# A cross-attention and state-space layer: loads before the main loop in another order, chunks of keys fetched seven ahead, the context's mean from longer rows

## The chip, the cores and the metric

The kernel runs on one core of a Trainium2 chip. The metric is the device time of one execution in microseconds (us); lower is better. The value before is the median of three runs. Where a stage is looked at, the figures come from one profiled execution, whose own time is given beside its span.

## The reference

The reference takes `x` (4096 rows of 512), a context `ctx` (3202 rows of 512), a second context `ctxb` (3202 rows of 64) and weights. All is float32. In short:

```python
xn  = layernorm(x, g1, beta1)
cn  = layernorm(ctx, g1, beta1)
q, k, v = heads(xn @ Wq.T + bq), heads(cn @ Wk.T + bk), heads(cn @ Wv.T + bv)   # 8 heads of 64
x1  = x + softmax(q @ k.T / 8) @ v @ Wo.T + b_o
u   = (layernorm(x1, g2, beta2) @ W_in.T + b_in) @ Bmat                          # 4096 x 64
s_t = silu(s_(t-1) @ A.T) + u_t                                                  # a scan over the rows
out = x1 + s @ Cmat + mean(ctxb, over its rows) @ W_prog.T + b_prog
```

The change concerns how `ctx`, `ctxb`, the weights and the first rows of `x` are brought in, before the attention proper starts.

## The kernel before, in words

The kernel has three stages: the preparation of K, V and the first block of Q; the attention, with the projections and the input of the scan as background work; and the scan with the output. The change lies in the first stage alone.

**Chunks and groups.** The context is cut into 26 chunks of 124 or 123 rows (`keys(c)`: 124 for the first four, 123 after), and chunks go in groups of four, so there are six full groups and one of two chunks. For each chunk, `load_chunk` brings the rows into a tile `cx` (SP's queue), `norm_chunk` takes its statistics on DVE (L111, L113), makes the scale and shift on POOL (L115 to L119) and the normalized rows `xh` on ACT (L125). `turn_chunk` transposes `xh` on TensorE (`tp_c`, L136) and copies it into the group's tile `ct`, by ACT for even chunks and by DVE for odd ones. Four pairs of matmuls make the V rows `pv` (L390); ACT copies them to `vs` (three buffers) and SP stores them to `vd` in DRAM (L400). After the last chunk of a group, four K products `pk` (L415) go through ACT to `ks` (three buffers, L423) and are stored by SP to `kd` (L428), two stores for each. The attention reads `kd` and `vd` back in tiles.

**Order.** The stage stands under `manual_schedule`, so each engine and each queue carries out its instructions in the order in which the program issues them. In iteration `c` the order is: load of chunk `c + 4`, normalization of chunk `c + 3`, V product of chunk `c`, transposes of chunk `c + 2`, copy and store of V of chunk `c`, and at a group's end the K products and stores. A load thus stands on SP's queue behind the V stores, and behind the K stores, that were issued before it. The tile `cx` has five buffers.

**Side work.** The generators `first` and `side` yield between small steps, and the loop takes a step of one of them in each iteration and after each K product (`next`). They fold the layer norm's gain and shift into the weights (`gain`, `shift`, `pr`, `pb`), fold `W_in` and `Bmat` into one matrix (`pw`, `pt`, `wc`), take the mean of `ctxb` (`cb`, `sums`, `pm`, `mean`), add constant rows (`rowb`, `modb`), and make the first block of Q (`queries(0)`: loads of `x`, `tp_x`, `pq`). Their loads go by ACT's queue, those of `x` by SP's. What is left of `side` after the loop is carried out there.

**Completion of loads and stores.** In the built program the loads and stores of both queues take eight completion semaphores in turn. An issue that takes a semaphore waits until the load or store that had it before is complete, whichever queue that one was on.

The lines that matter most: `load_chunk` (L345 to L350), the loads ahead of the loop (L366 to L374), the loop (L383 to L430), `fetch_w` (L199), the load of `ctxb` (L252 to L259) with its reduces (L305 to L313), the loads of `x` in `queries` (L155).

Of the kernel before, what the change touches and what calls it, by code (L numbers as in the profile page):

```python
# [8 lines left out]
F32 = mybir.dt.float32  # L9
# [3 lines left out]
ALU = mybir.AluOpType  # L13
# [10 lines left out]
GC = 4  # L24
# [21 lines left out]
def xattn_ssm_kernel(  # L46
# [97 lines left out]
    ps_m = actx.enter_context(tc.tile_pool(name="ps_m", bufs=2, space=PSUM))  # L144
    qt = {}

    def queries(Q):

        xns = []
        for half in range(2):  # L150
            xn = xnp.tile([P, NC, QU], F32, tag="xn", name=f"xn_{Q}_{half}")
            xns.append(xn)
            for t in range(NT // 2):
                r = Q * QB + half * QU + t * P
                xt = xp_.tile([P, H], F32, tag="x", name=f"x_{r}", bufs=3)  # L155
                nc.sync.dma_start(xt, x[r : r + P, :])
                yield False
                scaled = normalize(xt, P, f"x{r}", later=True)
                yield False
                yield False  # L160
                xh = scaled()
                yield False
                tp = transposes(ps_m, "m", xh, P, f"x{r}")
                yield True
                nc.scalar.copy(xn[:, :, t * P : (t + 1) * P], tp)
                yield False
                yield False
        for hp in range(NC):
            pq = ps_m.tile([P, 512], F32, tag="m", name=f"pq_{Q}_{hp}")
            for half in range(2):  # L170
                for i in range(NC):
                    nc.tensor.matmul(  # L172
                        pq[:, half * QU : (half + 1) * QU],
                        wq[:, i, hp * P : (hp + 1) * P],
                        xns[half][:, i, :],
                        start=(i == 0),
                        stop=(i == NC - 1),
                    )
            yield True
            t = qp.tile([P, QB], F32, tag="q", name=f"q_{Q}_{hp}")  # L180
            nc.scalar.activation(
                t, pq, AF.Identity, bias=bias[:, hp : hp + 1], scale=HD**-0.5
            )
            qt[Q, hp] = t
            yield False
# [10 lines left out]
    wv = wp.tile([P, NC, H], F32, name="wv")  # L196
    raw = [wp.tile([P, NC, H], F32, name=f"raw_{k}") for k in "qkv"]

    def fetch_w(k):  # L199
        nc.scalar.dma_start(raw[k], wsrc[:, :, k * H : (k + 1) * H])  # L200

    def gain(k, w):
        for i in range(NC):
            nc.vector.tensor_scalar(
                w[:, i, :], raw[k][:, i, :], g1s[:, i : i + 1], None, ALU.mult
            )
# [27 lines left out]


    def side():
        fetch_w(0)
        yield from shift(2)
        nc.scalar.dma_start(wo, wo_t.rearrange("(c p) o -> p c o", p=P))
        yield  # L240
        gain(0, wq)
        yield from shift(0)

        nc.vector.tensor_scalar(bias[:, :NC], bias[:, :NC], HD**-0.5, None, ALU.mult)

        win = wp.tile([P, NC, H], F32, name="win")
        nc.scalar.dma_start(win, w_in.rearrange("(c p) i -> p c i", p=P))
        bm = wp.tile([P, NC, NS], F32, name="bm")
        nc.scalar.dma_start(bm, bmat.rearrange("(c p) s -> p c s", p=P))
        bi = wp.tile([P, NC], F32, name="bi")  # L250
        nc.scalar.dma_start(bi, b_in)
        cb = wp.tile([CK, NCH, NS], F32, name="cb")  # L252
        a = GC * CK
        nc.scalar.dma_start(
            cb[:, :GC, :], ctxb[:a, :].rearrange("(c p) d -> p c d", p=CK)
        )
        nc.scalar.dma_start(
            cb[: CK - 1, GC:, :], ctxb[a:, :].rearrange("(c p) d -> p c d", p=CK - 1)
        )  # L259
        for _ in range(6):  # L260
            yield

        nc.scalar.dma_start(rowb, b_o.rearrange("(a h) -> a h", a=1).to_broadcast([P, H]))
        nc.scalar.dma_start(modb, b_prog.to_broadcast([P, H]))
        wp_t = wp.tile([NS, H], F32, name="wp_t")
        nc.scalar.dma_start(wp_t, wprog_t)
        for k in (0, NS):
            nc.scalar.dma_start(a_t[k : k + NS, k : k + NS], at)
        pw = ps_m.tile([P, 512], F32, tag="m", name="pw")
        for c in range(NC):  # L270
            nc.tensor.matmul(
                pw[:NS, :], bm[:, c, :], win[:, c, :], start=(c == 0), stop=(c == NC - 1)
            )
        yield
        wct = wp.tile([NS, H], F32, name="wct")
        nc.vector.tensor_copy(wct, pw[:NS, :])
        yield
        pt = ps_m.tile([P, NC, P], F32, tag="m", name="pt")
        for i in range(NC):
            nc.tensor.transpose(  # L280
                pt[:, i, :NS], wct[:, i * P : (i + 1) * P], ident[:NS, :NS]
            )
        yield
        wcr = wp.tile([P, NC, NS], F32, name="wcr")
        nc.vector.tensor_copy(wcr, pt[:, :, :NS])
        for i in range(NC):
            nc.vector.tensor_scalar(
                wc[:, i, :], wcr[:, i, :], g2s[:, i : i + 1], None, ALU.mult
            )
        yield  # L290
        pb = ps_m.tile([P, 512], F32, tag="m", name="pb")
        for c in range(NC):
            nc.tensor.matmul(
                pb[:NS, 0:1], bm[:, c, :], bi[:, c : c + 1], start=(c == 0), stop=False
            )
        for i in range(NC):
            nc.tensor.matmul(
                pb[:NS, 0:1], wcr[:, i, :], be2s[:, i : i + 1], start=False, stop=(i == NC - 1)
            )
        yield  # L300
        for k in (0, NS):
            nc.vector.tensor_copy(bu[k : k + NS], pb[:NS, 0:1])

        sums = wp.tile([CK, 2, NS], F32, name="sums")
        nc.vector.tensor_reduce(  # L305
            sums[:, 0, :], cb[:, :GC, :].rearrange("p c d -> p d c"), AX.X, ALU.add
        )
        nc.vector.tensor_reduce(
            sums[: CK - 1, 1, :],
            cb[: CK - 1, GC:, :].rearrange("p c d -> p d c"),  # L310
            AX.X,
            ALU.add,
        )  # L313
        yield
        pm = ps_m.tile([P, 512], F32, tag="m", name="pm")
        for i, n in enumerate((CK, CK - 1)):
            nc.tensor.matmul(
                pm[:NS, 0:1], sums[:n, i, :], ones[:n, 0:1], start=(i == 0), stop=(i == 1)
            )
        yield  # L320
        mean = wp.tile([NS, 1], F32, name="mean")
        nc.vector.tensor_scalar(mean, pm[:NS, 0:1], 1.0 / S2, None, ALU.mult)
        yield


        for dst, terms in (
            (modb, [(mean, wp_t)]),
            (rowb, [(bias[:, 2 * NC + c : 2 * NC + c + 1], wo[:, c, :]) for c in range(NC)]),
        ):
            pr = ps_m.tile([P, 512], F32, tag="m", name="pr")  # L330
            for i, (left, right) in enumerate(terms):
                nc.tensor.matmul(
                    pr, left.to_broadcast([left.shape[0], P]), right,
                    start=(i == 0), stop=(i == len(terms) - 1),
                )
            yield
            nc.vector.tensor_tensor(dst, pr, dst, ALU.add)
            yield
        yield from queries(0)

# [2 lines left out]
    def load_chunk(c):  # L345
        if c < NCH:
            n = keys(c)
            xt = cin.tile([CK, H], F32, tag="cx", name=f"cx_{c}", bufs=5)
            nc.sync.dma_start(xt[:n], ctx_in[key0(c) : key0(c) + n, :])
            cxs[c] = xt  # L350

# [13 lines left out]
    with tc.manual_schedule():  # L365
        load_chunk(0)  # L366
        nc.scalar.dma_start(g1s, g1)
        fetch_w(2)
        load_chunk(1)
        for t, src in ((be1s, beta1), (bqkv, b_qkv), (g2s, g2), (be2s, beta2)):  # L370
            nc.sync.dma_start(t, src)
        load_chunk(2)
        fetch_w(1)
        load_chunk(3)  # L374
        norm_chunk(0)
        norm_chunk(1)
        turn_chunk(0)
        gain(2, wv)
        turn_chunk(1)
        norm_chunk(2)  # L380
        work = side()
        first = shift(1)
        for c in range(NCH):  # L383
            load_chunk(c + 4)
            norm_chunk(c + 3)
            g, n = c // GC, keys(c)
            ct, o = cts[g], key0(c) - key0(g * GC)
# [13 lines left out]
                vd[:, c // 2, :n, c % 2, :].rearrange("h p d -> p h d"), vs[:n]  # L401
            )
            if c < GC:
                if c == 0:
                    gain(1, wk)
                next(first)
            else:
                next(work, None)
            if c % GC < GC - 1 and c < NCH - 1:
# [2 lines left out]
            for hp in range(NC):  # L412
# [13 lines left out]
                for b in range(g * GC, c + 1, 2):  # L426
                    m, k = 2 * keys(b), key0(b) - key0(g * GC)
                    nc.sync.dma_start(kd[hp, b // 2, :, :m], ks[:, k : k + m])  # L428
                for _ in range(2 if g > 2 else 1):
                    next(work, None)  # L430
        left = sum(1 for _ in work)
        assert left < 12, left
    prep.close()
    lctx = ExitStack()
    ps_s = lctx.enter_context(tc.tile_pool(name="ps_s", bufs=2, space=PSUM))
# [533 lines left out]
```

## Time and profile before

| | |
|---|---|
| time, median of three runs | 2682.13 us (2678.46 to 2682.83) |
| time of the profiled execution | 2679.33 us |
| its span in the profile | 2677.4 us |
| granted TensorE clock, mean | 0.977 of full speed |
| PE busy in the span | 2507.3 us, 94% |
| DVE, ACT, POOL busy | 80%, 69%, 77% |
| DMA, mean rate | 66 GB/s |
| first scores of the attention (L460) | at 304.84 us |

The profile gives, for each engine, the busy time; "busy tenths" show the span in 40 equal slices. PE is TensorE's matmuls and PEld its weight loads, DVE the vector engine, ACT the scalar engine, POOL GpSimd, SP the engine whose queue issues most of the loads and stores. A wait is named by who waited and for whom ("DVE st_c L111 <- DMA cx": the statistics waited for a chunk's load). `SPq` and `ACTq` are the issues on the two queues. The granted clock is what the throttle left of TensorE's full speed. The share of DMA is the mean over 16 engines.

### The profile page before, as it was taken

How to read it: one execution, taken by the hardware profiler on the slowest of the kernel's cores; microseconds unless marked ns; L12 is line 12 of the kernel's file. 1: busy time of each engine (PE TensorE's matmuls, PEld its weight loads, DVE VectorE, ACT ScalarE, POOL GpSimd, SP SyncE). 2: the span in 40 equal slices, each digit the busy share in tenths (PEclk: the TensorE clock that was granted, in tenths of full speed). 3: DMA queues.
4: the chain of work that ended last, by engine and by line, in shares of the span. 5: the costliest groups of instructions: out<-in, count | busy, mean ns of one | idle time of the engine just before them, and what ended most of it. 6: DMA issues, size and time to landing. Idle time of an engine off the chain costs nothing.

```text
span 2677.4 us, 44182 instructions
## 1 busy us (share of the span) xinstructions
PE 2507.3 (94%) x16588; PEld 1424.4 (53%) x16588; DVE 2146.1 (80%) x2321; ACT 1836.0 (69%) x2085; POOL 2065.1 (77%) x1170
## 2 busy tenths in 40 slices
PE   7788799999999999999999999999999999999957
PEld 3333555555565556555555556555555565555533
DVE  2121298899979998999989897999799979999825
ACT  2122387787878787877878787878687878788610
POOL 1111099899979998999979897999799979999870
PEclk9889999999999999999999999999999999999976
DMA  4332221112212221122111221212112211221043
GB/s 123 90 92 85 77 67 45 46 57 68 70 41 58 59 75 47 53 67 70 58 50 56 81 60 43 61 52 82 33 55 69 69 42 58 58 65 54 27 147 126
DMA packets 167551, 176.62 MB, mean 66 GB/s; under 512 B 16701, under 2 KB 140645, under 8 KB 167335
## 3 DMA queue, kind: packets, MB, share of 16 engines
q1 hardware_dynamic: 155374, 158.21, 20.0%
q10 hardware_dynamic: 11961, 15.54, 1.9%
q8 instruction: 134, 2.20, 0.3%
q14 instruction: 82, 0.67, 0.1%
HBM read 143.81 MB, written 29.89 MB: 65 GB/s over the span
## 4 chain that ended last, share of the span: by engine, by line
PE 44%; DVE 26%; issue 18%; ACT 8%; POOL 3%; DMA 2%; SPq 0%; ACTq 0%; DVEq 0%; POOLq 0%
DVE top L481 17%; PE s L460 14%; PE po L543 12%; DVE p L515 5%; PE pq L172 4%; ACT p L470 4%; PE pa L628 4%; ACT p L525 2%; PE tt L492 2%; PE py_c L871 1%; DVE rd L600 1%; PE mb L507 1%; PE pu L660 1%; PE pk L415 1%; POOL acc L534 1%
## 5 line engine op out<-in xcount | busy, mean ns | idle before, releaser
L534 POOL TENSOR_TENSOR acc<-p,acc 123x1024 f32<-123x1024 f32 x698 | 1657.0, 2374 | 115.3 <-ACT p L525 73.8
L470 ACT COPY p<-s 123x1024 f32<-123x1024 f32 (+1 forms) x832 | 834.2, 1003 | 274.1 <-PE s L460 263.4
L515 DVE TENSOR_TENSOR p<-p,mb 123x1024 f32<-123x1024 f32 (+1 forms) x832 | 1001.2, 1211 | 0.8 <-PE mb L507 0.8
L460 PE MATMUL s<-q,k 64*123 64x256 f32 (+1 forms) x6656 | 940.0, 401 | 61.0 <-DVE top L481 50.6
L525 ACT ACTIVATE p<-p 123x1024 f32<-123x1024 f32 (+1 forms) x832 | 880.1, 1058 | 143.7 <-DVE p L515 137.1
L481 DVE TENSOR_TENSOR top<-s,top 123x1024 f32<-123x1024 f32 x704 | 856.7, 1217 | 139.4 <-ACT p L470 130.6
L543 PE MATMUL po<-p,v 123*64 123x256 f32 (+1 forms) x6656 | 901.3, 392 | 1.1 <-ACT o L586 0.9
L460 PEld LDWEIGHTS s<-q,k 64*123 64x123 f32 (+1 forms) x6656 | 559.3, 181 | 373.6 <-DVE top L481 172.5
L543 PEld LDWEIGHTS po<-p,v 123*64 123x64 f32 (+1 forms) x6656 | 404.8, 136 | 399.4 <-issue 223.1
L534 POOL TENSOR_TENSOR acc<-p,p 124x1024 f32<-124x1024 f32 x64 | 151.9, 2374 | 152.6 <-ACT p L525 152.3
L115 POOL TENSOR_SCALAR ve_c<-mv_c 123x1 f32<-123x1 f32 (+1 forms) x26 | 6.1, 233 | 187.7 <-DVE mv_c L113 181.6
L111 DVE BATCH_NORM_STATS2 st_c<-cx 123x6 f32<-123x512 f32 (+1 forms) x26 | 18.0, 692 | 151.8 <-DMA cx<-in_ctx_dram 151.8
L628 PE MATMUL pa<-wo,o 128*128 128x512 f32 x256 | 119.5, 611 | 2.3 <-DVE x L637 2.3
L172 PE MATMUL pq<-xn,wq 128*128 128x256 f32 x512 | 117.9, 383 | 0.0
L481 DVE TENSOR_TENSOR top<-s,p 124x1024 f32<-124x1024 f32 x64 | 77.9, 1217 | 40.6 <-DMA k<-kd 39.3
L125 ACT ACTIVATE xh_c<-cx,nmr_c,rstd_c 123x512 f32<-123x512 f32 (+1 forms) x26 | 21.1, 812 | 129.1 <-POOL nmr_c L119 129.1
L172 PEld LDWEIGHTS pq<-xn,wq 128*128 128x128 f32 x512 | 95.0, 190 | 20.7 <-issue 6.3
L415 PE MATMUL pk<-ct,wk 128*128 128x492 f32 (+2 forms) x224 | 99.0, 599 | 3.3 <-ACT ks L423 3.3
L390 PE MATMUL pv<-wv,ct 128*123 128x512 f32 (+1 forms) x208 | 96.3, 607 | 0.0
L589 POOL TENSOR_TENSOR both<-acc 124x512 f32<-124x512 f32 x63 | 80.8, 1283 | 4.9
L499 DVE TENSOR_REDUCE m<-tt 128x2 f32<-128x496 f32 x128 | 79.9, 665 | 0.7 <-PE tt L492 0.7
L628 PEld LDWEIGHTS pa<-wo,o 128*128 128x128 f32 x256 | 46.8, 192 | 62.2 <-issue 56.3
(157 smaller groups left out, 1335.3 us busy)
## 6 DMA issues: line engine op xcount, KB each, us to landing
k<-kd SPq DMA_DIRECT2D x352, 123.0 KB
v<-vd SPq DMA_DIRECT2D x352, 123.0 KB
x<-in_x_dram SPq DMA_DIRECT2D x32, 256.0 KB
xr<-in_x_dram SPq DMA_DIRECT2D x32, 256.0 KB
out_dram<-row_c ACTq DMA_DIRECT2D x32, 256.0 KB
k<-kd SPq DMA_DIRECT2D x64, 124.0 KB
v<-vd SPq DMA_DIRECT2D x64, 124.0 KB
x1d<-x SPq DMA_DIRECT2D x28, 256.0 KB
```

The costliest lines, as they stand in the source:

```text
L172: nc.tensor.matmul(pq[:, half * QU : (half + 1) * QU], wq[:, i, hp * P : (hp + 1) * P], xns[half][:, i, :], start=(i == 0), stop=(i == NC ...
L390: nc.tensor.matmul(pv[:n, :H], ct[:, i, o : o + n], wv[:, i, :], start=(i == 0), stop=(i == NC - 1),)
L415: nc.tensor.matmul(pk[:, :n_g], wk[:, i, hp * P : (hp + 1) * P], ct[:, i, :n_g], start=(i == 0), stop=(i == NC - 1),)
L460: nc.tensor.matmul(s[:n, a, b, :], kts[(*w["at"][:2], c)][r, b * n : (b + 1) * n], q[r], start=True, stop=True,)
L470: nc.scalar.copy(t[:n], s[:n])
L481: nc.vector.tensor_tensor(w["top"][:n], s[:n], before[:n], ALU.max)
L515: nc.vector.tensor_tensor(t[:n], t[:n], w["mb"][:n].unsqueeze(2).to_broadcast([n, 2, 2, QU]), ALU.subtract,)
L525: nc.scalar.activation(t[:n], t[:n], AF.Exp)
L534: nc.gpsimd.tensor_tensor(w["acc"][:n], t[:n], before[:n], ALU.add)
L543: nc.tensor.matmul(w["po"][a * HD : (a + 1) * HD, 0, :], vts[(*w["at"][:2], c)][:n, b, a * HD : (a + 1) * HD], t[:n, a, b, :], start=(c == ...
L589: nc.gpsimd.tensor_tensor(both, acc[:, :, 0, :], acc[:, :, 1, :], ALU.add)
L628: nc.tensor.matmul(pa, o_t[Q, c][:, t * P : (t + 1) * P], wo[:, c, :], start=(c == 0), stop=(c == NC - 1),)
```

## The change

W_v is loaded in two halves, one by each queue. The chunks 1 to 3 and W_k are issued at once, the four small vectors after them, and chunks 4 to 6 ahead of the loop; in the loop, iteration `c` loads chunk `c + 7`, and `cx` has eight buffers. The gain of W_v stands ahead of the statistics of chunk 1, and gain and shift of W_k come one chunk later. The loads of `win`, `bm` and `bi` move ahead, that of `wo` later. `ctxb` is read as 128 partitions of 25 successive rows (6.4 KB each), with the last two rows in a tile of their own, and one reduce takes the place of two. The first 512 rows of `x` come in one load by ACT. The side work takes two steps after each K product from group 2 on, and is done when the loop ends.

```diff
@@ queries @@
-    def queries(Q):
+    def queries(Q, fetched=None):
...
-                xt = xp_.tile([P, H], F32, tag="x", name=f"x_{r}", bufs=3)
-                nc.sync.dma_start(xt, x[r : r + P, :])
-                yield False
+                if fetched:
+                    xt = fetched[:, half * (NT // 2) + t, :]
+                else:
+                    xt = xp_.tile([P, H], F32, tag="x", name=f"x_{r}", bufs=3)
+                    nc.sync.dma_start(xt, x[r : r + P, :])
+                    yield False
...
@@ fetch_w @@
-    def fetch_w(k):
-        nc.scalar.dma_start(raw[k], wsrc[:, :, k * H : (k + 1) * H])
+    def fetch_w(k, queue, part=slice(0, NC)):
+        queue.dma_start(raw[k][:, part], wsrc[:, part, k * H : (k + 1) * H])
...
@@ side @@
-        fetch_w(0)
+        fetch_w(0, nc.scalar)
         yield from shift(2)
-        nc.scalar.dma_start(wo, wo_t.rearrange("(c p) o -> p c o", p=P))
-        yield
-        gain(0, wq)
-        yield from shift(0)
-
-        nc.vector.tensor_scalar(bias[:, :NC], bias[:, :NC], HD**-0.5, None, ALU.mult)
 
         win = wp.tile([P, NC, H], F32, name="win")
         nc.scalar.dma_start(win, w_in.rearrange("(c p) i -> p c i", p=P))
...
-        cb = wp.tile([CK, NCH, NS], F32, name="cb")
-        a = GC * CK
-        nc.scalar.dma_start(
-            cb[:, :GC, :], ctxb[:a, :].rearrange("(c p) d -> p c d", p=CK)
-        )
-        nc.scalar.dma_start(
-            cb[: CK - 1, GC:, :], ctxb[a:, :].rearrange("(c p) d -> p c d", p=CK - 1)
-        )
-        for _ in range(6):
-            yield
+        gain(0, wq)
+        yield from shift(0)
+
+        cb = wp.tile([P, S2 // P, NS], F32, name="cb")
+        a = S2 // P * P
+        nc.scalar.dma_start(cb, ctxb[:a, :].rearrange("(p c) d -> p c d", p=P))
+        cb2 = wp.tile([S2 - a, NS], F32, name="cb2")
+        nc.scalar.dma_start(cb2, ctxb[a:, :])
+        x0 = wp.tile([P, NT, H], F32, name="x0")
+        yield
+
+        nc.vector.tensor_scalar(bias[:, :NC], bias[:, :NC], HD**-0.5, None, ALU.mult)
...
             nc.scalar.dma_start(a_t[k : k + NS, k : k + NS], at)
+        yield
+        nc.scalar.dma_start(wo, wo_t.rearrange("(c p) o -> p c o", p=P))
         pw = ps_m.tile([P, 512], F32, tag="m", name="pw")
...
-        sums = wp.tile([CK, 2, NS], F32, name="sums")
-        nc.vector.tensor_reduce(
-            sums[:, 0, :], cb[:, :GC, :].rearrange("p c d -> p d c"), AX.X, ALU.add
-        )
-        nc.vector.tensor_reduce(
-            sums[: CK - 1, 1, :],
-            cb[: CK - 1, GC:, :].rearrange("p c d -> p d c"),
-            AX.X,
-            ALU.add,
-        )
+        sums = wp.tile([P, NS], F32, name="sums")
+        nc.vector.tensor_reduce(sums, cb.rearrange("p c d -> p d c"), AX.X, ALU.add)
+        nc.scalar.dma_start(x0, x[:QB, :].rearrange("(t p) h -> p t h", p=P))
         yield
         pm = ps_m.tile([P, 512], F32, tag="m", name="pm")
-        for i, n in enumerate((CK, CK - 1)):
+        for i, t in enumerate((sums, cb2)):
+            n = t.shape[0]
             nc.tensor.matmul(
-                pm[:NS, 0:1], sums[:n, i, :], ones[:n, 0:1], start=(i == 0), stop=(i == 1)
+                pm[:NS, 0:1], t, ones[:n, 0:1], start=(i == 0), stop=(i == 1)
             )
...
-        yield from queries(0)
+        yield from queries(0, x0)
@@ load_chunk @@
-            xt = cin.tile([CK, H], F32, tag="cx", name=f"cx_{c}", bufs=5)
+            xt = cin.tile([CK, H], F32, tag="cx", name=f"cx_{c}", bufs=8)
...
@@ ahead of the loop, and the loop @@
         load_chunk(0)
         nc.scalar.dma_start(g1s, g1)
-        fetch_w(2)
+        fetch_w(2, nc.scalar, slice(0, NC // 2))
+        fetch_w(2, nc.sync, slice(NC // 2, NC))
         load_chunk(1)
+        load_chunk(2)
+        fetch_w(1, nc.scalar)
+        load_chunk(3)
         for t, src in ((be1s, beta1), (bqkv, b_qkv), (g2s, g2), (be2s, beta2)):
             nc.sync.dma_start(t, src)
-        load_chunk(2)
-        fetch_w(1)
-        load_chunk(3)
+        for c in range(4, 7):
+            load_chunk(c)
         norm_chunk(0)
-        norm_chunk(1)
         turn_chunk(0)
         gain(2, wv)
+        norm_chunk(1)
         turn_chunk(1)
         norm_chunk(2)
         work = side()
         first = shift(1)
         for c in range(NCH):
-            load_chunk(c + 4)
+            load_chunk(c + 7)
             norm_chunk(c + 3)
...
             if c < GC:
-                if c == 0:
+                if c == 1:
                     gain(1, wk)
-                next(first)
+                for _ in range((0, 1, 1, 2)[c]):
+                    next(first)
             else:
                 next(work, None)
...
-                for _ in range(2 if g > 2 else 1):
+                for _ in range(2 if g > 1 else 1):
                     next(work, None)
```

More of the change, by code (lines that the diff above doesn't have):

```diff
@@ L428, in xattn_ssm_kernel @@
                     nc.sync.dma_start(kd[hp, b // 2, :, :m], ks[:, k : k + m])
-                for _ in range(2 if g > 2 else 1):
+                for _ in range(2 if g > 1 else 1):
                     next(work, None)
         left = sum(1 for _ in work)
-        assert left < 12, left
+        assert left == 0, left
     prep.close()
```

## The prediction

> **What bounds the kernel now.** Read first the page's slices (40 of 67 us each: busy tenths, granted clock, DMA).
>
> ```profile
> PE   7788799999999999999999999999999999999957
> ...
> PEclk9889999999999999999999999999999999999976
> DMA  4332221112212221122111221212112211221043
> ```
>
> TensorE is at nine tenths from slice 6 on; the first four slices and a half, the preparation of K, V and the first Q, stand at 7 to 8. The diff touches only these. The PE timeline puts the first scores (L460) at 304.84 us. All before is the stage in question: PE is busy 247.0 us of it and idle 57.8. The 2372.6 us after it are taken as they are. Next the windows view, cut at the group borders (group = four chunks of keys: V, then K). Columns: window, length, busy us of PE, PEld, DVE, ACT, POOL with counts, granted clock, DMA share, GB/s.
>
> ```profile
> 17.07:58.60 41.53, 40.75 (x116) 17.82 (x117) 10.13 (x23) 9.33 (x15) 6.68 (x18) 1.00 0.33 101
> 58.60:96.40 37.80, 35.44 (x97) 15.66 (x96) 7.03 (x17) 7.99 (x13) 4.68 (x12) 0.95 0.40 124
> 96.40:155.30 58.90, 40.33 (x109) 17.76 (x107) 6.40 (x16) 9.93 (x17) 4.21 (x12) 0.86 0.31 88
> 155.30:197.50 42.20, 38.11 (x100) 17.26 (x100) 10.11 (x19) 9.58 (x16) 5.27 (x15) 0.92 0.25 81
> 197.50:234.85 37.35, 32.17 (x86) 15.07 (x85) 4.77 (x10) 9.59 (x16) 4.21 (x12) 0.91 0.27 86
> 234.85:278.50 43.65, 35.05 (x105) 17.88 (x104) 5.49 (x12) 11.11 (x18) 5.27 (x15) 0.96 0.25 75
> 278.50:304.80 26.30, 24.08 (x97) 18.01 (x96) 0.00 (x0) 5.35 (x10) 0.00 (x0) 1.00 0.15 44
> ```
>
> Group 2 (third row) takes 58.9 us at 0.86 clock, the others about 40. Who keeps PE idle: the list of waits, 0 to 330 us (total, times, longest).
>
> ```profile
> DVE st_c L111 <- DMA cx<-in_ctx_dram: 151.8, 23, 20.7
> ...
> PE tp_c L136 <- ACT xh_c L125: 42.6, 9, 10.6
> ...
> ACT ks L423 <- DMA bi<-in_L_xattn_b_in_dram: 9.4, 1, 9.4
> ```
>
> So: chunk load, then stats (DVE), POOL, ACT, then PE's transposes. Why are loads late? The DVE timeline shows chunks 16, 17, 18:
>
> ```profile
> 163.28 0.70 DVE L111 BATCH_NORM_STATS2 st_c<-cx 123x6 f32<-123x512 f32 x1 [4.44 <-DMA cx<-in_ctx_dram]
> ...
> 170.49 0.69 DVE L111 BATCH_NORM_STATS2 st_c<-cx 123x6 f32<-123x512 f32 x1 [5.67 <-DMA cx<-in_ctx_dram]
> ...
> 177.64 0.69 DVE L111 BATCH_NORM_STATS2 st_c<-cx 123x6 f32<-123x512 f32 x1 [6.13 <-DMA cx<-in_ctx_dram]
> ```
>
> One chunk lands every 7.15 us while PE needs 3.86 us for it (V matmuls start at 96.41, 100.27, 104.12). The DMA queue over 164 to 178 us (packets, MB, share of 16 engines), and SP's own waits:
>
> ```profile
> q1 hardware_dynamic: 1198, 0.99, 20.7%
> ```
>
> ```profile
> SPq L400 <- DMA cb<-in_ctxb_2048x_dram: 14.8, 1, 14.8
> ```
>
> A share of about 3/16 throughout, at 70 GB/s: three engines carry the chunk load and the V store.
>
> [...] `cb` is read in 256-byte pieces[...]; 4037 packets under 512 B pass between 92 and 132 us, and the window there has the long wait above. [...] after 8.09 us idle a V product took 4.86 us for 3.60.
>
> **Prices.** Chunk load 3.36 us of the three engines (chunks 3 and 4 land at 21.74 and 25.10, back to back), V store 7.15 − 3.36 = 3.8, landing latency 2.4 (an x load takes 3.1 from issue to use[...]). [...]
>
> **The change, part by part.**
>
> *Start.* W_v by two queues, chunks 1 to 3 and W_k at once instead of W_k at 7.44. The engines carry the same bytes until chunk 1, which still gates PE's second transpose: raw_v lands at about 10, chunk 1 at 13 (now 13.55). Gain 0.7 us; bounds −2 and +2 (W_k ahead in line). If W_v came after chunk 1, DVE would hold the stats of chunk 1 behind `gain`, which now stands ahead of them: that is the +2. The four small vectors now wait for chunk 0, W_v and `g1`; all are in by about 10, and they are first read at 23. SP's chunks 4 to 6 stand behind them: no loss, the engines are busy with chunks 2 and 3. `gain` and `shift` of W_k go one chunk later: the same 1.6 us on DVE and 3.6 + 1.0 on PE, costed at nothing, since the first K product is due only at 39 and W_k is in by 13; V products of chunks 1 to 3 cover them. If W_k came after 30, PE would wait in the `shift` by as much.
>
> *Context's mean.* [...] From issue (99) to SP's release (128.8) that load held chunks 12 to 14 back. Its reduces cost DVE 0.6 + 2.56 us; one of 1600 elements at the same rate costs 2.9. Group 2 loses its 18.6 us of idling (58.90 − 40.33).
>
> *Seven ahead.* A load is now issued four iterations before its stats instead of one. PE then pays its own work only: per chunk 3.86, per K product 3.35, plus the side work where the built program puts it. Group 0: 39.5 (41.53 less 0.78 idle and 1.3 of slow clock). Group 1: 4 x 3.86 + 4 x 3.35 = 28.8, shift of W_q 4.5 and `pw` 3.6: 36.9. Group 2: 28.8 and 7.3 (`pt`, `pb`, `pm` 1.8, the two `pr` 5.5): 36.1. Groups 3 and 4: 28.8 and two transposes of x: 29.8 each. The first Q product: 3.45. Group 5: 28.8 and three Q products 10.4: 39.2. Group 6: two V products 6.9, four short K products 6.6: 13.5. Sum 228.3. With a start at 17.3 and 2.3 for the first K load the scores begin at **247.9**, 57 us earlier. That is the floor: 39.6 us of idling (57.8 less 16 at the start and 2.3 at the end) and some 17 of slow clock (247.0 busy less 228.3, and 1 to 2 at the start that stay).
>
> *What is late next.* Four pairs and eight K stores hold the three engines 28.6 + 2.7 = 31.3 us a group. To the end of group 0 they have eleven loads: chunk 3 is through at 15.7, then 7 x 3.36 + 4 x 3.8 + W_q 2.8 + 2.7 and the landing 2.4 make 62; PE is done at 57. Group 1 adds `win`, `bm`, `cb` (6): 37.4 against 36.9. Group 2 adds `wo`, `rowb`, `modb`, `wp_t`, x (7.4): 38.7 against 36.1. Group 3: 31.3 against 29.8. The loads bear this, with four chunks in hand. The stores do not quite: SP is in order, so the first K store of a group issues behind its last V store, and the fourth `ks` (three buffers) waits for it on ACT, with `xh` of the chunk PE turns 7.7 us into the next group behind it. SP's lag, 5 to 9 us, passes that slack (7.7 less 1.6 for `ks` and `xh`) in groups 2 to 4 by 0 to 4 us each. Group 1 has a wait of its own: ACT issues `modb`, whose completion semaphore (eight go round) is that of V store 7, and `a_t`, that of the first K store. ACT stops at about 84 until 98, and `ks`, then `xh` of chunk 11 stand behind it: 2 us of PE. I take 8 us of stalls and 3 of slow clock. Bounds: 0, if they fit the slack, and 33 (second case).
>
> *x in one load.* 1 MB by ACT, in group 2, for four loads by SP: 2.8 us of the engines either way. PE's waits for x (6.9 us, in the idling above) go; four SP places at 0.44 go; ACT pays one issue, 0.4 us. `wo`, moved later, is read at the end of group 2, some 20 us after its issue; `win`, `bm`, `bi`, moved earlier, are read 25 us after theirs: nothing, with the V products of their group as cover.
>
> Sum: −57 + 11 = **−46 us**. The profiled execution took 2679.33 us, 1.93 beyond its span; the median of the runs is 2682.13, 0.1% above. Forecast 2682.1 − 46 = **2636**.
>
> **Rivals.**
>
> *The stores stay the bound.* SP waits for each `ks` in turn (kd stores take 13.2 us of SP in group 0), so loads and K phase would not overlap: 28.6 + 13.2 = 41.8 us in groups 1 to 3, 38.5 in group 4, then PE's 42.7 and 13.5. Scores at 58 + 125.4 + 38.5 + 56.2 + 2.3 = 280: −24, **2658**. For it: today's periods of 37 to 44. Against: today the loads are needed one iteration after issue; afterwards the engines can drain queued loads in the K phase.
>
> *ACT stands still* (slower). Five batches of loads on ACT each wait for a DMA eight places before, perhaps queued behind loads that nobody needs yet. Eight outstanding at 3.6 us are 29 us; less 8 of slack, 21 a time. Three such (63) outweigh 57 and leave 2682 + 6 = **2688**. For it: the 9.4 us wait for `bi` now. [...] It decides when ACT's blocks beyond the slack pass 57 us.
>
> *Nothing gained*: all stalls reappear in front of the stores; **2682**.
>
> **Numbers.** First case 0.68, stores 0.25, ACT 0.05, nothing 0.02. A measurement of this kernel can tell about 0.2% (5 us) from no change: faster 0.93, same 0.02, slower 0.05. Range 2622 (the floor and 3 us of scatter) to 2664 (the stores' case and 6).
>
> **What would show it.** Right: first scores at 255 to 262; no `cb` in SP's waits; group 2 near 40 us; DVE's wait for `cx` far below 151.8; clock near 1 from 96 to 220. ACT's `ks` waits for DMA should grow. Wrong: groups 1 to 3 still near 41 us with a DMA share of 0.19 throughout (the stores), ACT idle 20 us at a time before `ks` (third case), or a stage after the first scores that differs from 2372.6 us by over 5.

## The result, and the profile after

| | before | after |
|---|---|---|
| median of six runs, us | 2680.57 (2675.43 to 2685.05) | 2642.82 (2633.27 to 2649.38) |
| ratio, 95% interval | | 0.9858 (0.9834 to 0.9883) |
| profiled execution, its span | 2679.33, 2677.4 | 2643.80, 2642.0 |
| first scores of the attention | 304.84 (L460) | 263.32 (L459) |
| PE busy and idle ahead of them | 247.0, 57.8 | 234.0, 29.3 |
| stage after them | 2372.6 | 2378.7 |

The change makes the kernel faster by 1.4%. In the profiled executions the preparation is 41.5 us shorter: 28.5 us less of idle TensorE and 13.0 us less of busy time for the same products, at a granted clock of 0.99 where it was 0.94. These are the windows of the preparation, before and then after (columns as in the prediction: length; busy us of PE, PEld, DVE, ACT, POOL with counts; clock, DMA share, GB/s):

```profile
0.00:304.84 304.84, 247.02 (x707) 120.20 (x707) 47.52 (x107) 65.84 (x106) 33.54 (x97) 0.94 0.31 91
```

```profile
0.00:263.32 263.32, 233.97 (x707) 115.61 (x707) 46.27 (x106) 66.57 (x106) 32.87 (x97) 0.99 0.33 105
```

Next the page's slices of the kernel after (66 us each: busy tenths, granted clock, DMA).

```profile
PE   7989899999999999999999999999999999999857
...
PEclk9999999999999999999999999999999999999966
DMA  3422221112212121222112211222121312221133
```

The clock's first four digits were 9, 8, 8 and 9 and are all 9 now. The last two slices hold the end with the scan, which the diff doesn't touch; in the clock they are at 6 and 6 where they were at 7 and 6. The windows of the preparation after, cut at the group borders:

```profile
19.28:60.04 40.76, 40.76 (x113) 17.40 (x113) 12.22 (x29) 9.17 (x14) 6.71 (x18) 1.00 0.34 114
60.04:97.34 37.30, 37.30 (x106) 16.09 (x105) 6.10 (x15) 8.23 (x13) 4.47 (x14) 1.00 0.39 120
97.34:133.79 36.45, 35.78 (x115) 16.96 (x114) 10.76 (x23) 9.24 (x15) 4.18 (x12) 1.00 0.45 143
133.79:171.12 37.33, 31.87 (x90) 14.77 (x89) 6.08 (x15) 11.05 (x18) 8.30 (x24) 0.95 0.26 85
171.12:208.12 37.00, 33.61 (x106) 17.23 (x105) 5.30 (x12) 11.05 (x18) 5.30 (x15) 1.00 0.31 99
208.12:247.12 39.00, 39.00 (x130) 22.66 (x128) 2.12 (x4) 10.65 (x17) 1.06 (x3) 1.00 0.19 58
247.12:263.32 16.20, 13.67 (x50) 8.90 (x48) 0.00 (x0) 3.71 (x7) 0.00 (x0) 1.00 0.27 78
```

Group 2 (third row) went from 58.9 us to 36.45. Rows 1, 2 and 6 have PE busy for their whole length: the chunk loads no longer bound them. What idling is left stands in rows 4 and 5 and at both ends. The list of waits of the kernel after, 0 to 300 us (total, times, longest):

```profile
ACT ks L422 <- DMA kd<-ks: 33.6, 4, 14.9
...
PE tp_c L136 <- ACT xh_c L125: 21.2, 4, 11.0
...
DVE st_c L111 <- DMA cx<-in_ctx_dram: 13.4, 4, 6.8
...
PE tp_x L136 <- ACT xh_x L125: 5.0, 4, 1.5
```

DVE's wait for chunks fell from 151.8 to 13.4 us, and in its place ACT now waits for K stores, 33.6 us. In front of `tp_c` PE paid little for that: of its 21.2 us there, 17.3 are the two transposes ahead of the first product (11.05 and 6.26), so 3.9 us remain in groups 3 and 4.

The stage after the first scores has the same code in both. It took 6.1 us more in this execution, most of it in its last 580 us, where the granted clock was 0.92 against 0.93. These two rows are the windows of the end, before and then after:

```profile
2100.00:2677.00 577.00, 516.68 (x3361) 290.63 (x3359) 458.36 (x539) 362.89 (x427) 452.93 (x250) 0.93 0.23 71
```

```profile
2060.00:2642.00 582.00, 520.21 (x3364) 292.29 (x3361) 458.37 (x539) 363.27 (x427) 453.61 (x250) 0.92 0.23 70
```

The 64 output matmuls of the scan (`py_c`) alone took 35.3 us against 31.8. Why the clock differs there is open. The six spans after run from 2631.4 us at a mean clock of 0.984 to 2647.5 at 0.978. So below, parts of the preparation are compared by the time of the first scores, one profile each, and whole kernels by times and ratios; where there is one run, its time alone says little.

The first scores have a scatter of their own. The first V product starts at 17.32 to 17.95 us in the four kernels whose start is that of before, and at 18.64 to 19.28 in the five whose start is that of after; it lasts 4.69 to 6.14 us in these nine. So a difference of some 2 us or less in the first scores (an estimate from these ranges) tells nothing.

### The profile page after: what moved, and what is told of

The parts are those of the page before. It is cut to its first block, busy times and chain, and to the rows that moved or that the text cites. A ratio compares the mean times of both kernels' runs of the same rounds, so it can differ in the third digit from the quotient of the medians.

```text
span 2642.0 us, 44166 instructions
## 1 busy us (share of the span) xinstructions
PE 2498.9 (95%) x16588; PEld 1422.2 (54%) x16588; DVE 2144.1 (81%) x2320; ACT 1837.8 (70%) x2085; POOL 2066.3 (78%) x1170
## 4 chain that ended last, share of the span: by engine, by line
PE 50%; DVE 27%; issue 11%; ACT 7%; POOL 2%; DMA 1%; SPq 1%; ACTq 0%; DVEq 0%; POOLq 0%
DVE top L480 17%; PE s L459 14%; PE po L542 12%; DVE p L514 5%; PE pq L175 4%; ACT p L469 4%; PE pa L627 4%; PE pv L388 3%; PE pk L414 3%; ACT p L524 2%; PE tt L491 2%; PE py_c L870 1%; DVE rd L599 1%; PE mb L506 1%; PE pu L659 1%
## 5 line engine op out<-in xcount | busy, mean ns | idle before, releaser
L459 PE MATMUL s<-q,k 64*123 64x256 f32 (+1 forms) x6656 | 941.4, 402 | 61.2 <-DVE top L480 49.4
L459 PEld LDWEIGHTS s<-q,k 64*123 64x123 f32 (+1 forms) x6656 | 560.2, 182 | 374.3 <-DVE top L480 169.3
L358 DVE COPY ct<-tp_c 128x492 f32<-128x492 f32 (+1 forms) x13 | 8.7, 671 | 127.8 <-PE tp_c L136 127.8
L422 ACT ACTIVATE ks<-pk,bias 128x492 f32<-128x492 f32 (+2 forms) x28 | 18.0, 643 | 111.8 <-PE pk L414 63.6
L414 PE MATMUL pk<-ct,wk 128*128 128x492 f32 (+2 forms) x224 | 89.2, 550 | 0.0
```

Source lines behind the costliest of these rows:

```text
L414: nc.tensor.matmul(pk[:, :n_g], wk[:, i, hp * P : (hp + 1) * P], ct[:, i, :n_g], start=(i == 0), stop=(i == NC - 1),)
L459: nc.tensor.matmul(s[:n, a, b, :], kts[(*w["at"][:2], c)][r, b * n : (b + 1) * n], q[r], start=True, stop=True,)
```

## The experiments

The theory under test was the prediction's: chunk loads and V stores take the time of some three of the 16 DMA engines (its estimate from their mean share, 20.7% of 16 from 164 to 178 us), the mean's load and the short lead each make PE wait, and one load of `x` in place of four is worth PE's 6.9 us of waits for `x` and no more. The rivals: the lead is worth little because the stores bind (second case), ACT stands at its own loads (third case), or the gain is due to `x`.

**The mean's rows alone**, on the kernel before:

```diff
-        cb = wp.tile([CK, NCH, NS], F32, name="cb")
+        cb = wp.tile([P, S2 // P, NS], F32, name="cb")
...
+        nc.scalar.dma_start(cb, ctxb[:a, :].rearrange("(p c) d -> p c d", p=P))
```

> The kernel before with one part of the change: the second context read as 128 rows of 6.4 KB (and one reduce). First scores were at 304.8 us before, 263.3 after the whole change. If the 256-byte pieces on three DMA engines held the chunk loads back, group 2 (58.9 us) comes down to about 41 and the first scores come at 284 to 290; the time falls by some 18 us. If the gap in group 2 was the order of the loads and not the engines' time, the first scores stay above 298.

Measured: first scores at 290.75 us, 14.1 earlier; 2667.34 us, ratio 0.9943 (0.9926 to 0.9961). The scores miss the expected range by 0.75 us, and the time falls by 15.1 us where some 18 were expected. Group 2 takes 42.05 us (V products at 98.32 and 140.37) where it took 58.90: the old form of this load did hold the chunks back, though the length of its pieces and the number of its rows changed together. In the kernel before, from 108 to 124 us, with this load under way, the mean share of the 16 DMA engines was 0.22 at 65 GB/s, 13.3% by SP's queue and 8.3% by ACT's; that it was three engines is an estimate from such shares. DVE still waits 134.1 us for chunks.

**Seven chunks ahead alone**, on the kernel before:

```diff
-            xt = cin.tile([CK, H], F32, tag="cx", name=f"cx_{c}", bufs=5)
+            xt = cin.tile([CK, H], F32, tag="cx", name=f"cx_{c}", bufs=8)
...
-        load_chunk(3)
+        for c in range(3, 7):
+            load_chunk(c)
...
-            load_chunk(c + 4)
+            load_chunk(c + 7)
```

> The kernel before with one part of the change: eight chunk buffers, chunks 4 to 6 loaded ahead of the loop, chunk c + 7 loaded in iteration c; the second context as before. If the lead covers only lateness and the three engines still have to move the 256-byte pieces[...], the first scores come at 280 to 290. If the lead covers that too, they come at 263 to 268, and the mean's new form is worth nothing beside it.

Measured: first scores at 298.69, only 6.2 earlier; 2674.26 us, ratio 0.9968 (0.9955 to 0.998). That missed both expectations. Its list of waits, 0 to 300 us:

```profile
ACT ks L424 <- DMA cx<-in_ctx_dram: 20.6, 1, 20.6
...
PE tp_x L136 <- ACT xh_x L125: 18.1, 3, 8.1
...
PE pk L416 <- ACT ks L424: 17.6, 1, 17.6
...
ACT ks L424 <- DMA cb<-in_ctxb_2048x_dram: 14.9, 1, 14.9
...
DVE st_c L111 <- DMA cx<-in_ctx_dram: 13.4, 5, 5.7
```

and ACT's timeline (start, length, queue or engine, line):

```profile
119.43 7.48 ACTq L263 DMA_DIRECT2D rowb<-in_L_xattn_b_o_dram  x1
126.94 0.46 ACTq L264 DMA_DIRECT2D modb<-in_L_xattn_b_prog_dram  x1
127.44 0.53 ACTq L266 DMA_DIRECT2D wp_t<-in_L_xattn_W_prog_dram  x1
136.69 3.83 ACTq L268 DMA_DIRECT2D a_t<-in_L_xattn_A_dram  x2
140.62 1.23 ACT L424 ACTIVATE ks<-pk,bias 128x492 f32<-128x492 f32 x2 [20.62 <-DMA cx<-in_ctx_dram]
```

The lead did what it was for: DVE's wait for chunks is 13.4 us. But ACT was held up in its side loads from 119.43 until 140.52, `ks` stood behind them, and PE behind `ks` for 17.6 us. That is the prediction's third case, at the 21 us a time that it named, in a kernel that still has the old `cb`. It isn't the only loss: in front of `tp_x` PE waits 18.1 us, where it was 6.9 before. In all PE idles 57.3 us ahead of the first scores, against 57.8, so nearly all of the gain is shorter busy time.

**Mean and lead together**, on the kernel before (both diffs above):

> The kernel before with the two large parts only: the mean's rows of 6.4 KB and the lead of seven chunks; x still in four loads at their former places. If the lead puts x behind a trailing SP queue, this ends where the changed kernel with four loads of x did, at 283 to 290 us to the first scores. If the two parts are all there is, at 263 to 268.

Measured: first scores at 286.61; 2665.45 us in one run. This is the expected range for `x` behind a trailing SP queue. The two parts bring 18.2 us; 23.3 us of the whole change are still missing. The waits name the place:

```profile
DVE st_x L111 <- DMA x<-in_x_dram: 46.7, 4, 13.7
...
PE tp_x L136 <- ACT xh_x L125: 18.4, 3, 8.1
```

The four loads of `x` now come late. Before the change PE waited 6.9 us for `x` in the whole stage.

**The change with a lead of four**:

```diff
-            xt = cin.tile([CK, H], F32, tag="cx", name=f"cx_{c}", bufs=8)
+            xt = cin.tile([CK, H], F32, tag="cx", name=f"cx_{c}", bufs=5)
...
-        for c in range(4, 7):
-            load_chunk(c)
...
-            load_chunk(c + 7)
+            load_chunk(c + 4)
```

> The changed kernel with the lead undone: five buffers, chunk c + 4 loaded in iteration c. If a chunk every 7.15 us behind its own V store is what starved TensorE, the groups go back to about 40 us and the first scores to 285 to 292, waits of the statistics for chunks above 100 us. If the start and the x load carried the gain, they stay below 275.

Measured: first scores at 283.56, so 20.2 us of the gain are lost, a little less than expected; 2660.90 us, ratio to before 0.9922 (0.9905 to 0.9939). DVE's wait for chunks is back:

```profile
DVE st_c L111 <- DMA cx<-in_ctx_dram: 144.3, 21, 15.8
```

So the lead, added to the rest, is worth 20.2 us, and added to the kernel before 6.2. The parts don't add.

**The change with `x` in four loads by SP**, at their former places in `queries` (whose steps among the side work come back with them), the rest as after:

```diff
-        nc.scalar.dma_start(x0, x[:QB, :].rearrange("(t p) h -> p t h", p=P))
...
-        yield from queries(0, x0)
+        yield from queries(0)
```

> The changed kernel with the first rows of x in four loads by SP again. If the chunk lead makes up for SP's place, the first scores stay at 263 to 266; if the four loads cost what they did (6.9 us of TensorE's waits for x), they come at about 270.

Measured: first scores at 288.54, 25.2 us later than after; 2669.61 us in one run. That missed both expectations. SP's timeline shows when the load is issued:

```profile
122.95 6.04 SPq L342 DMA_DIRECT2D cx<-in_ctx_dram  x1
129.08 1.03 SPq L396 DMA_DIRECT2D vd<-vs  x1
130.20 12.17 SPq L425 DMA_DIRECT2D kd<-ks  x8
142.43 0.44 SPq L159 DMA_DIRECT2D x<-in_x_dram  x1
```

and DVE's what stands behind it:

```profile
147.17 0.69 DVE L111 BATCH_NORM_STATS2 st_x<-x 128x6 f32<-128x512 f32 x1 [15.86 <-DMA x<-in_x_dram]
...
182.49 0.69 DVE L111 BATCH_NORM_STATS2 st_x<-x 128x6 f32<-128x512 f32 x1 [18.81 <-DMA x<-in_x_dram]
```

SP trails: the issue of `x` comes behind all eight K stores of group 2. DVE stands at `st_x` for 15.9 and 18.8 us, with the statistics of the next chunks behind it. PE waits with them:

```profile
151.64 1.08 PE L136 MATMUL tp_c<-ident,xh_c 123*128 123x123 f32 x4 [10.47 <-ACT xh_c L125]
...
185.63 1.12 PE L136 MATMUL tp_x<-ident,xh_x 128*128 128x128 f32 x4 [12.82 <-ACT xh_x L125]
```

PE's idle time in the stage is 49.8 us against 29.3, and its busy time 4.8 us longer: 25.2. This kernel has all of the change but `x`, and comes no earlier than mean and lead together (286.61): without `x` the other moves of loads and side work show no gain.

**Four loads by SP, but early**: issued where the change issues its one load, into the same tile.

```diff
-        nc.scalar.dma_start(x0, x[:QB, :].rearrange("(t p) h -> p t h", p=P))
+        for t in range(NT):
+            nc.sync.dma_start(x0[:, t, :], x[t * P : (t + 1) * P, :])
```

> The changed kernel with the first rows of x in four loads on SP's queue, but issued where the change issues the one load, so that the side work keeps its steps. With the four loads at their former places the first scores came at 288.5 us instead of 263.3, and the statistics waited for x behind K stores. If the place on SP's queue is the cause, they come at 263 to 267 here. If the queue (SP instead of ACT) or the number of loads is, they stay above 275.

Measured: first scores at 263.51 (after: 263.32); 2639.98 us in one run. SP issues the four loads ahead of the K stores of group 2:

```profile
129.27 7.40 SPq L308 DMA_DIRECT2D x<-in_x_dram  x4
136.77 7.84 SPq L428 DMA_DIRECT2D kd<-ks  x8
```

To within the scatter neither the queue nor the number of loads matters; their place in the order does.

**W_k behind the four small vectors**, the rest as after:

```diff
-        fetch_w(1, nc.scalar)
         load_chunk(3)
...
+        fetch_w(1, nc.scalar)
         for c in range(4, 7):
```

> The changed kernel with W_k issued behind the four small vectors instead of beside chunk 1. If W_k in line ahead of chunk 1 made the start later (first V product 19.28 us after the change, 17.95 before), that product starts at 17 to 17.8 and the first scores come 1.5 to 2.5 us earlier (261 to 262). If chunk 1 was late for another reason, it stays at 19 and nothing moves.

Measured: first V product at 18.49 us (after: 19.28), first scores at 260.74, 2634.95 us in one run. Chunk 1's statistics begin at 14.46 instead of 15.25, but the other four kernels with the start of the change have them at 14.61 to 14.80. So W_k ahead of chunk 1 costs at most 0.8 us and perhaps 0.2, less than was expected and not to be told from scatter; of the 2.6 us in the first scores, 1.1 are a shorter first V product (4.77 us for 5.83).

**Five `ks` buffers**, the rest as after:

```diff
-                ks = cin.tile([P, GC * CK], F32, tag="ks", name=f"ks_{g}_{hp}")
+                ks = cin.tile([P, GC * CK], F32, tag="ks", name=f"ks_{g}_{hp}", bufs=5)
```

> The changed kernel with five buffers for ks instead of three. If the fourth ks of a group waits for the first K store, and TensorE behind it, then ACT's 33.6 us of waits for kd go, TensorE's waits at 144 and 179 us go, and the first scores come at 255 to 258. If the three engines are the bound behind it, the stall comes back as a late V store or chunk, and they stay above 261.

Measured: first scores at 253.46, 9.9 us earlier than after; 2626.10 us in one run. ACT's waits for `kd` are gone, and of PE's stalls between the first V product and the last K product only three remain, 0.65, 1.46 and 1.46 us. This wait stays in the list:

```profile
ACT ks L422 <- DMA modb<-in_L_xattn_b_prog_dram: 13.8, 1, 13.8
```

It costs PE nothing. Of the 9.9 us, 6.2 are idling and 3.7 busy time of PE. Not all of it is the buffers': 0.5 us are an earlier start and 1.1 a shorter first V product (4.69 us for 5.83), which lie in the scatter; 8.2 us are gained behind that product.

**Chunk loads of 128 rows**, the rest as after. Rows beyond the chunk are loaded and not read; the computation is unchanged. The two cases are that a chunk lands sooner for the number of its rows, and that it doesn't.

```diff
-            xt = cin.tile([CK, H], F32, tag="cx", name=f"cx_{c}", bufs=8)
-            nc.sync.dma_start(xt[:n], ctx_in[key0(c) : key0(c) + n, :])
+            xt = cin.tile([P, H], F32, tag="cx", name=f"cx_{c}", bufs=8)
+            m = min(P, S2 - key0(c))
+            nc.sync.dma_start(xt[:m], ctx_in[key0(c) : key0(c) + m, :])
```

> The changed kernel with each chunk loaded as 128 rows (the last one as 123), of which only the chunk's own are used. [...] chunks land in some 3 us instead of 6, the queue stops trailing, ACT's waits for kd shrink, the start comes 2 to 4 us earlier, and the first scores come at 249 to 255. [...] nothing moves: 262 to 264.

Measured: first scores at 247.74, 15.6 us earlier than after; 2624.41 us, ratio to before 0.9796 (0.9772 to 0.982). From PE's timeline, first V product and first scores:

```profile
12.52 5.46 PE L389 MATMUL pv<-wv,ct 128*124 128x512 f32 x8
...
247.74 0.48 PE L460 MATMUL s<-q,k 64*124 64x256 f32 x2 [2.57 <-DMA k<-kd]
```

More bytes, and sooner, by more than was expected: the first V product comes 6.8 us earlier (expected 2 to 4), and ACT's waits for `kd` fall from 33.6 to 2.8 us. Behind the first product 8.4 us are gained, as much as five `ks` buffers gain. Chunk 0 is issued at 0.72 us and its statistics begin at 3.49, where they began at 7.90 after the change (issued at 0.73), and the page's first slice, of some 66 us, moves 151 GB/s, where it was 124. How many engines serve one load no view shows by itself. In the kernel after, the mean share of the 16 engines is 19.9% at 74 GB/s from 20 to 24 us, with only SP's queue and its chunk loads under way, and 88.5% for ACT's queue from 8 to 10 us, where a load of weights over 128 rows is under way (366 GB/s with SP's 13.2%): the time of some 3 and some 14 engines, by an estimate from these shares.

**128 rows, with V stores of 112 rows and the rest**:

```diff
-            nc.sync.dma_start(
-                vd[:, c // 2, :n, c % 2, :].rearrange("h p d -> p h d"), vs[:n]
-            )
+            for r0, r1 in ((0, 112), (112, n)):
+                nc.sync.dma_start(
+                    vd[:, c // 2, r0:r1, c % 2, :].rearrange("h p d -> p h d"), vs[r0:r1]
+                )
```

> As the 128-row kernel, and each V store split in 112 rows[...] and the other 11 or 12. If three engines hold the V store, V stores leave the way too: first scores at 247 to 251, ACT's waits for kd near zero. If the extra issue on SP costs more than the engines gain, they come later than with 128 rows alone.

Measured: first scores at 246.53; 2623.36 us, ratio 0.9788 (0.976 to 0.9815). The first scores lie 1.2 us earlier, in the scatter, and the intervals overlap almost wholly: no gain that can be told.

**All cures**: 128 rows, five `ks` buffers and W_k later; then the split V stores as well.

> The changed kernel with 128-row chunk loads, five buffers for ks and W_k behind the four small vectors. The three came to 15.6, 9.9 and 2.6 us of earlier first scores one by one. If they cure one lateness, the first scores come at 243 to 247, little below the 128 rows alone (247.7); if they add, at 236 to 240. TensorE's own work puts the floor at 12.3 + 228.3 + 2.3 = 243.

> As the last, with each V store in 112 rows and the rest. The V store on its own on three engines takes 3.8 us of the 3.86 that TensorE needs for a chunk. If that still delays anything, the first scores come 1 to 3 us earlier than in the last; if not, the same within 1 us.

Measured: first scores at 247.73 and 248.27; 2623.73 us, ratio 0.9775 (0.9761 to 0.9789), and 2620.48 us, ratio 0.9777 (0.9759 to 0.9795). They beat before and after (the intervals lie below that of after), but not the 128 rows alone by anything measurable. The first misses its range for one lateness (243 to 247) by 0.7 us and is far from the one for a sum (236 to 240): the 128 rows and the buffers cure the same waits. With 128 rows the scores already stand 4.6 us from a floor of 12.52 + 228.3 + 2.3 = 243.1 (the prediction's sum for PE after that kernel's own start), so nothing is left for the others to save. (The 3.8 us of a V store in the second expectation are the prediction's estimate, 7.15 − 3.36.)

## Why the prediction was right, and where it was not

The total: 2636 forecast, 2642.82 measured, inside the range. In the profiled execution it is 2633.3 against 2643.8. Of these 10.5 us, 6.1 lie in the untouched stage and 4.4 in the preparation (scores at 258.9, with the stalls taken, against 263.32). Of the 4.4, 2.0 are the start (19.28 for 17.3) and 1.3 group 0. The sums take 2.8 us for a load of 1 MB, 2.7 for eight K stores of 123 KB and 2.4 for the landing. These are estimates that fit the kernel before: it moved 372 GB/s from 92 to 94 us, at which 1 MB takes 2.8 us, eight such stores 2.7 and 256 KB of `x` 0.7 of the 3.1 from issue to use.

**Own work of PE: right.** Groups 0 to 2 and 5 took 40.76, 37.30, 36.45 and 39.00 us for 39.5, 36.9, 36.1 and 39.2. Group 0's excess is the first V product, 5.83 us where the sum took 3.60, though it says that 1 to 2 us of slow clock at the start stay (the granted clock of this window reads 1.00 all the same). The sum has a slip the other way: group 0 was measured from 17.07 us, where a transpose begins, but the start of 17.3 is that of the V product 0.9 us behind it, so these 0.9 us are in it twice. The PE timeline, with stalls of interest:

```profile
19.28 5.83 PE L388 MATMUL pv<-wv,ct 128*124 128x512 f32 x8
...
144.23 0.64 PE L136 MATMUL tp_c<-ident,xh_c 123*128 123x123 f32 x4 [2.98 <-ACT xh_c L125]
145.88 0.66 PE L136 MATMUL tp_x<-ident,xh_x 128*128 128x128 f32 x4 [1.02 <-ACT xh_x L125]
146.38 5.29 PE L388 MATMUL pv<-wv,ct 128*123 128x512 f32 x8
...
164.02 0.66 PE L136 MATMUL tp_x<-ident,xh_x 128*128 128x128 f32 x4 [1.46 <-ACT xh_x L125]
...
263.32 0.92 PE L459 MATMUL s<-q,k 64*124 64x256 f32 x6 [2.53 <-DMA k<-kd]
```

**What is late next: right in mechanism, and in its sum partly by luck.** 8 us of stalls and 3 of slow clock were taken. Groups 3 and 4 took 37.33 and 33.54 us (the fifth row less the first Q product, 3.46) for 29.8 each: 11.3 over, of which 8.9 are idle and the rest, 2.4, longer busy time (granted clock 0.95 in group 3, 1.00 in group 4). ACT's timeline shows both waits that were named:

```profile
99.93 0.33 ACTq L263 DMA_DIRECT2D modb<-in_L_xattn_b_prog_dram  x1
...
102.16 0.67 ACT L422 ACTIVATE ks<-pk,bias 128x492 f32<-128x492 f32 x1 [14.33 <-PE tp_c L136]
...
142.80 0.67 ACT L422 ACTIVATE ks<-pk,bias 128x492 f32<-128x492 f32 x1 [14.87 <-DMA kd<-ks]
```

ACT stands in group 1 until 102 (98 was named), and PE pays nothing for it where 2 us were taken. The fourth `ks` waits at 142.80 for the store, and the `tp_c` at 144.23 behind it stalls 2.98 us; in group 4 the like stall is 0.90, in group 5 none (0 to 4 each was said; the lag and slack given there make 0 to 3). With 1.02 us in front of the `tp_x` behind each, these stalls are 5.9 us, and with the 2.4 of longer busy time 8.3; five buffers gained 8.2. The other 2.9 us weren't in the sum: two `tp_x` wait 1.46 us each for rows that ACT normalizes behind a `ks`, and they stay with five buffers. Slow matmuls stand behind short stalls too: in the kernel before, behind a single one of 2.58 us (173.69, `tp_c`), the two matmuls of `pr` took 2.07 us, with a granted clock of 0.53 from 173.6 to 177 us, where they took 1.12 after the change without a stall.

**The mean: mechanism right, size plausible.** Group 2's 18.6 us of idling are 0.67 in the whole change; alone the part brings 14.1, and added to the lead 12.1. The whole change with the old load wasn't run. The one reduce took what was said:

```profile
115.75 2.89 DVE L306 TENSOR_REDUCE sums<-cb 128x64 f32<-128x1600 f32 x1
```

**Seven ahead: right only together with the rest.** The sum priced all parts together and gave the lead no price of its own. Alone it brought 6.2 us, since ACT stood still at its loads and `x` came late; in the whole, 20.2.

**x in one load: the weakest step.** It was given the 6.9 us that PE waited in front of `tp_x`, a size of the queue as it was. With the lead SP trails by a K phase, and four loads left at their old places, with their steps, would have cost 25.2 us. The total came out because the sum was made upwards from PE's own work, and so assumed `x` in time. The 6.9 us didn't go either: 5.0 remain, behind `ks` and no longer behind the load.

**Start: wrong, and open.** 0.7 us earlier was taken, 1.3 later measured. W_v came as said (`gain` at 10.84 for "about 10"), but chunk 1's statistics began at 15.25 instead of 13. The five kernels with this start have them at 14.61 to 15.25, the four with the old one at 12.91 to 13.55, so the delay is no scatter. W_k explains little of it: without it ahead of chunk 1 they begin at 14.46. A half of W_v now stands ahead of chunk 1 on SP's queue; W_v by one queue in the new order wasn't tried.

**The signs that were named.** First scores at 263.32 for 255 to 262: 1.3 late. No `cb` among SP's waits, group 2 at 36.45, the clock near 1 outside group 3 (0.95), ACT's `ks` waits grown: as said. The stage after differs by 6.1 us, where over 5 was named as a sign of being wrong; that bound was too narrow, since the spans of this one kernel differ by 16 us. The stores' case fell by groups 1 and 2 at 37.30 and 36.45 (41.8 was its number).

## What to carry to other kernels

When loads are issued further ahead, look at every other load that shares their in-order queue: what stood well enough in a queue that keeps up comes a whole phase late in one that trails. Sum a pipelined stage upwards from the bounding engine's own work, and then price each wait by experiment in the final kernel, since a part's worth depends on the others (6.2 or 20.2 us for the same edit). Count the rows of a transfer before its bytes: four or five more rows per chunk were worth 15.6 us here, and two more `ks` buffers, which cure a part of the same waits, about 8.

## What the runs showed of the hardware that was not expected

Issuing is not always short, and it depended on the rows of the loads. After the change three chunk loads in a row at the start, of 124 rows each, hold SP for 4.29 us, and a vector's load behind them for 5.85; with 128 rows the same issues take 1.42 and 0.33. Which mechanism holds SP, no run shows. And an engine that computes and issues loads can stand still at them for long: ACT was idle 14.33 us around `modb` in the kernel after and 20.62 us with the lead alone. That the first is a wait for the completion semaphore of a V store is read from the order of the built program; no run shows it by itself.
